# A transformer block's last stage: first inputs prepared in the stage before, inputs two tiles ahead, and the last tile turned on TensorE

## The chip, the cores and the metric

One core of a Trainium2 chip runs the whole program. Its engines have instruction streams of their own, each executed in order, and wait for one another by semaphores: TensorE (PE; its weight loads are shown apart as PEld), VectorE (DVE), ScalarE (ACT), GpSimd (POOL) and SyncE (SP), which here only issues DMAs. The metric is the device time of one execution in microseconds (us). Before the change it is 3047.3 us, the median of three runs (3041.62 to 3050.27).

## The reference

The input x has 128 sequences of 32 tokens with 512 features, 4096 tokens in all. Three residual steps follow one another, each on a layer norm of x: cross attention to 257 context rows, a delta-rule attention with a gated MLP, and a feed-forward network (FFN) on rotated and quantised values. The change lies in the last one. Its core:

```python
def act_quant(x):
    scale = 127.0 / jnp.clip(jnp.max(jnp.abs(x), axis=-1, keepdims=True), EPS)
    return jnp.clip(jnp.round(x * scale), -128.0, 127.0) / scale
def h_bitlinear(x, w):
    return jnp.einsum('bsh,oh->bso', act_quant(fwht(x)), weight_quant(w))
gate = h_bitlinear(hidden_states, w_gate)
up = h_bitlinear(hidden_states, w_up)
return h_bitlinear(jax.nn.silu(gate) * up, w_down)
```

fwht is a normalised Walsh-Hadamard rotation over the features (512 going in, 2048 before w_down); weight_quant gives weights of -1, 0 and 1 times one scale. The result is added to x.

## The kernel before

The program is a row of stages; intermediate results go through DRAM. Cross attention writes x1 and, beside its own work, the quantised FFN weights as bf16 (fq). The delta attention follows, then delta_out_mlp in 16 blocks of 256 tokens. Its function mlp makes gate and up products (L823, L826) and the down product (L834), adds the residual (L839) and stores x2 (L841). It also starts the FFN: it takes the mean off x2, applies the two upper levels of the rotation with additions (butterflies, L126 and L127) and stores the result as z2 (L846); the variance stays in mv2. A function solving(b) gives further work to deal out beside the MLP block b; it comes from beside_mlp, which hands out parts of the delta rule's substitution until they are used up. The function mixed deals out the steps of several lists by the share of their costs that is done. The function behind makes DVE instructions of such steps follow the MLP's last marked DVE instruction.

hadamard_ffn is the last stage, 32 tiles of 128 tokens. It opens its pools after the MLP: weights wg and wu (bf16, 16 KB a partition each) on the right side of SBUF, which the substitution used before, and wd beside them. PSUM has one pool of eight banks, named ps, for all products of the stage. One tile i goes through these steps:

- load brings z2 (tile zt, L932); turned transposes it on PE (L97, four 128x128 blocks) and copies it to SBUF on ACT (zT, L970);
- rotated multiplies each block with the 128x128 Hadamard matrix hd (L939), which ends the rotation;
- integers finds the largest magnitude (L976), makes the scale qs (L948, L950, L951), rounds by adding and subtracting a large constant (t on ACT, L956; q on DVE, L960) and makes the factors f (L981);
- integers_turned transposes q by a DMA from SP (qT, L986);
- middle computes, for each of four groups of 512 columns, the gate and up products (L996, L999), silu on ACT (s, L1001) and their product on DVE (m, L1002);
- butterflies applies the upper four levels of the 2048-wide rotation on DVE, eight operations of 128x1024;
- middle_turned transposes m on PE and copies it on ACT (mT, L1009); rotated follows for each group (four banks, pr);
- last_integers finds the maxima (L1016, L1020), the scale (L948 to L951), and rounds each group with two ACT operations (t L956, q L958); last_turned transposes q2 by DMA (q2T, L1031);
- finish makes the down product (L1037, bank pd), scales it on ACT (xo, L1039), adds x2 by an accumulating DMA from POOL (L1040) and stores the result from SP (L1041).

The loop over i interleaves tiles. In iteration i it does: load of tile i+3, turned of i+1, the first group of middle of i, rotated and integers of i+1, finish of i-3, the other three groups of middle of i, middle_turned, rotated and last_integers of i-1, and butterflies of i. Before the loop, tile 0 is turned, rotated, rounded and transposed. The planner of the framework takes this order as a priority; where an instruction isn't ready by its estimates, it puts a later one ahead of it on the same engine. So small DVE operations, which depend on one another, have butterflies of another tile between them.

Of the kernel before, what the change touches and what calls it, by code (L numbers as in the profile page):

```python
# [10 lines left out]
FP = mybir.dt.float32  # L11
BF = mybir.dt.bfloat16
# [684 lines left out]
def delta_out_mlp(  # L697
# [14 lines left out]
    with stack:  # L712
# [177 lines left out]
        for b in range(NBL):  # L890
            mixed(
                (3.5 * FC + 9.5 * NTL, mlp(b)),
                (16.0, back(b + 1) if b + 1 < NBL else None),
                (2.0, part(late, 2.0)),
                *((cost, behind(tc, mark, steps)) for cost, steps in solving(b)),
            )


def hadamard_ffn(g: Ctx, x2, z2, mv2, had, ffn, out):


    tc, nc = g.tc, g.nc
    c1, c2 = 1.0 / math.sqrt(D), 1.0 / math.sqrt(IF)
    NG = IF // D
    stack, (st, xp, wk1, mp1, wk, mp, ps) = pools(
        tc, ("d_st", 6), ("d_x", 4), ("d_wk1", 3), ("d_m1", 2), ("d_wk", 3), ("d_m", 2),
        ("d_ps", 8, PSUM),
    )
    right = dict(bufs=1, side="right", reuse_waits="tile")
    with tc.tile_pool(name="d_w", **right) as wp, tc.tile_pool(name="d_w2", **right) as wp2, stack:  # L910
        hd = wp.tile([P, P], FP, name="hd")
        nc.sync.dma_start(hd, had)
        w = []
        for i, (dst, sc) in enumerate(ffn):
            w.append(((wp, wp, wp2)[i].tile([P, IF * D // P], BF, name=f"wq{i}"), sc))
        (wg, sg), (wu, su), (wd, sd) = w
        for t, (dst, _) in zip((wg, wu), ffn):
            nc.sync.dma_start(t, dst)
        wg = wg.rearrange("p (c n) -> p c n", c=DC)
        wu = wu.rearrange("p (c n) -> p c n", c=DC)  # L920
        wd = wd.rearrange("p (c n) -> p c n", c=IC)
        magic = wp.tile([P, 1], FP, name="magic")
        nc.vector.memset(magic, MAGIC)
        minus = wp.tile([P, 1], FP, name="minus")
        nc.vector.memset(minus, -MAGIC)
        both = wp.tile([P, 2], FP, name="both")
        nc.vector.tensor_copy(both[:, 0:1], sg)
        nc.vector.tensor_copy(both[:, 1:2], su)

        def load(i, src, name):  # L930
            t = xp.tile([P, D], FP, name=name)
            nc.sync.dma_start(t, src[i * P : (i + 1) * P, :])  # L932
            return t

        def rotated(xT, c0):

            pr = ps.tile([P, D], FP, name="ps")
            for c in range(DC):
                nc.tensor.matmul(  # L939
                    pr[:, c * P : (c + 1) * P], xT[:, c0 + c, :], hd, start=True, stop=True  # L940
                )
            return pr

        def scales(mx, c):


            m = st.tile([P, 1], FP, name="m")
            nc.vector.tensor_scalar(m, mx, c, Q_EPS, ALU.mult, ALU.max)  # L948
            qs = st.tile([P, 1], FP, name="qs")
            nc.vector.reciprocal(qs, m)  # L950
            nc.vector.tensor_scalar(qs, qs, c, 127.0, ALU.mult, ALU.mult)  # L951
            return m, qs

        def rounded(q, pr, qs, scalar=False):
            t = wk.tile([P, D], FP, name="t")
            nc.scalar.activation(t, pr, AF.Identity, bias=magic, scale=qs)  # L956
            if scalar:
                nc.scalar.activation(q, t, AF.Identity, bias=minus)  # L958
            else:
                nc.vector.tensor_scalar(q, t, MAGIC, None, ALU.subtract)  # L960

        def statistics(ns):

            nc.scalar.activation(rstd[:, ns], mv2[:, ns, 1], AF.Sqrt, bias=g.ln_eps)
            nc.vector.reciprocal(rstd[:, ns], rstd[:, ns])
            nc.vector.tensor_scalar_mul(rstd[:, ns], rstd[:, ns], c1)

        def turned(i):
            zT = wk1.tile([P, DC, P], FP, name="zT")
            nc.scalar.copy(zT, g.transposed(ps, z.pop(i), g.ident))  # L970
            return zT

        def integers(i, pr):

            mx = st.tile([P, 1], FP, name="mx")
            nc.vector.tensor_reduce(mx, pr, AX.X, ALU.max, apply_absolute_value=True)  # L976
            m, qs = scales(mx, rstd[:, i : i + 1])
            q = wk1.tile([P, D], BF, name="q")
            rounded(q, pr, qs)
            f = st.tile([P, 2], FP, name="f")  # L980
            nc.vector.tensor_scalar_mul(f, both, m)  # L981
            return q, f

        def integers_turned(q, f):
            qT = wk1.tile([P, DC, P], BF, name="qT")
            nc.sync.dma_start_transpose(qT, q)  # L986
            return qT, f

        def middle(qT, f):

            m = mp.tile([P, IF], FP, name="m")
            for k in range(NG):
                ks = slice(k * D, (k + 1) * D)
                pg = ps.tile([P, D], FP, name="ps")
                for dc in range(DC):
                    nc.tensor.matmul(pg, qT[:, dc, :], wg[:, dc, ks], start=dc == 0, stop=dc == DC - 1)  # L996
                pu = ps.tile([P, D], FP, name="ps")
                for dc in range(DC):
                    nc.tensor.matmul(pu, qT[:, dc, :], wu[:, dc, ks], start=dc == 0, stop=dc == DC - 1)  # L999
                s = wk.tile([P, D], FP, name="s")  # L1000
                nc.scalar.activation(s, pg, AF.Silu, scale=f[:, 0:1])  # L1001
                nc.vector.scalar_tensor_tensor(m[:, ks], pu, f[:, 1:2], s, ALU.mult, ALU.mult)  # L1002
                yield m

        def middle_turned(m):
            mT = mp.tile([P, IC, P], FP, name="mT")
            for k in range(NG):
                pt = g.transposed(ps, m[:, k * D : (k + 1) * D], g.ident)
                nc.scalar.copy(mT[:, k * DC : (k + 1) * DC, :], pt)  # L1009
            return mT  # L1010

        def last_integers(pr):

            mx = st.tile([P, NG], FP, name="mx4")
            for k in range(NG):
                nc.vector.tensor_reduce(  # L1016
                    mx[:, k : k + 1], pr[k], AX.X, ALU.max, apply_absolute_value=True
                )
            mx1 = st.tile([P, 1], FP, name="mx")
            nc.vector.tensor_reduce(mx1, mx, AX.X, ALU.max)  # L1020
            mm, qs = scales(mx1, c2)
            q = mp1.tile([P, IF], BF, name="q2")
            for k in range(NG):
                rounded(q[:, k * D : (k + 1) * D], pr[k], qs, True)
            f = st.tile([P, 1], FP, name="fd")
            nc.vector.tensor_mul(f, mm, sd)
            return q, f

        def last_turned(q):
            qT = mp1.tile([P, IC, P], BF, name="q2T")  # L1030
            nc.sync.dma_start_transpose(qT, q)  # L1031
            return qT

        def finish(i, qT, f):
            pd = ps.tile([P, D], FP, name="ps")
            for c in range(IC):
                nc.tensor.matmul(pd, qT[:, c, :], wd[:, c, :], start=c == 0, stop=c == IC - 1)  # L1037
            xo = wk.tile([P, D], FP, name="xo")
            nc.scalar.activation(xo, pd, AF.Copy, scale=f)  # L1039
            nc.gpsimd.dma_start(xo, x2[i * P : (i + 1) * P, :], accum_op=ALU.add)  # L1040
            nc.sync.dma_start(out[i * P : (i + 1) * P, :], xo)  # L1041

        n = NT // P
        late = n - NTL
        rstd = wp.tile([P, n], FP, name="rstd")
        z = {i: load(i, z2, "zt") for i in range(3)}
        nc.sync.dma_start(wd.rearrange("p c n -> p (c n)"), ffn[2][0])
        statistics(slice(0, late))  # L1050
        f, m, q, done = integers_turned(*integers(0, rotated(turned(0), 0))), {}, {}, {}
        for i in range(n + 3):
            if i + 3 < n:
                z[i + 3] = load(i + 3, z2, "zt")
            if i + 1 < n:
                zT = turned(i + 1)
            if i < n:
                steps = middle(*f)
                m[i] = next(steps)
            if i == n // 2:  # L1060
                statistics(slice(late, n))
            if i + 1 < n:
                f = integers_turned(*integers(i + 1, rotated(zT, 0)))
            if 0 <= i - 3:
                finish(i - 3, *done.pop(i - 3))
            if i < n:
                for _ in steps:
                    pass
# [119 lines left out]
```

## Time and profile before

| what | us |
|---|---|
| median of three runs | 3047.3 (3041.62 to 3050.27) |
| profiled execution, its own time | 3042.59 |
| its span | 3040.8 |
| PE busy in the span | 2895.6 |
| DVE busy | 2010.3 |
| ACT busy | 1052.8 |
| POOL busy | 664.0 |

The profile comes from one execution. Busy time is the union of an engine's instructions; a matmul's end is modelled, so a full PE is not PE at its peak. A line number is that of the kernel's source; L97 is the helper transposed, and what it writes and reads tells which step it is. In a timeline row, start and duration stand first, then engine, line, operation, output and input with shapes; the bracket gives the idle time before it and what ended that. Rows of the same kind in a row are merged, with their count. The granted clock of PE is a share of full speed.

### The profile page before, as it was taken

The page shows a single profiled execution, that of the slowest core. Times are in us where ns is not written, and L with a number is a line of the kernel's source. Part 1 is how long each engine was busy: PE and PEld are TensorE (multiplying, and loading weights), DVE is VectorE, ACT ScalarE, POOL GpSimd, SP SyncE. Part 2 cuts the span into 40 slices and gives each one's busy share as a digit, 9 for nine tenths or more (in the row PEclk, how much of TensorE's full clock was granted, in tenths as well). Part 3 has the DMA queues.
Part 4 walks back from the last instruction along what each step waited for, and adds up shares of the span by engine and source line. Part 5 has one row for each costly group of instructions (what it writes and reads, how often), then busy time and mean ns, then how long its engine had stood idle before and what let it go on. Part 6 is the DMA issues. An engine that isn't in the chain of part 4 may idle for free.

```text
span 3040.8 us, 40815 instructions
## 1 busy us (share of the span) xinstructions
PE 2895.6 (95%) x14856; PEld 1647.0 (54%) x14918; DVE 2010.3 (66%) x3368; ACT 1052.8 (35%) x1780; POOL 664.0 (22%) x963
## 2 busy tenths in 40 slices
PE   8999999999999999599999999999999899999996
PEld 3444444443333333276666677776667666666664
DVE  2453534326699797368787877878522299989995
ACT  1111111215656666422111221112112156666664
POOL 1121212112686675321211110101000000000000
PEclk9999999999999999799999999999999999999998
DMA  9897998863554544641414132231311123344433
GB/s 331 278 309 267 320 308 311 281 215 96 170 147 128 174 132 123 200 137 58 132 54 127 57 119 82 74 99 42 128 52 46 56 60 77 77 82 83 82 66 65
DMA packets 344248, 428.99 MB, mean 141 GB/s; under 512 B 152304, under 2 KB 254832, under 8 KB 340592
## 3 DMA queue, kind: packets, MB, share of 16 engines
q1 hardware_dynamic: 307824, 326.19, 35.7%
q0 software_dynamic: 36224, 100.19, 10.8%
q8 instruction: 119, 1.95, 0.3%
q14 instruction: 81, 0.66, 0.1%
HBM read 288.36 MB, written 93.85 MB: 126 GB/s over the span
## 4 chain that ended last, share of the span: by engine, by line
PE 38%; issue 23%; DVE 4%; DMA 2%; POOL 1%; ACT 0%; SPq 0%; POOLq 0%; DVEq 0%; ACTq 0%
PE pm L823 8%; PE pm L826 8%; PE pm L834 8%; PE pp L520 5%; PE ps L797 4%; PE pg L455 2%; PE ps L764 2%; DVE W L442 1%; DVE pr L436 1%; DMA xs<-x 1%; POOL xo L1040 1%; DMA wd<-in_WdownT_dram 1%; PE ps L97 1%; PE pm L455 0%; PE pn L579 0%
## 5 line engine op out<-in xcount | busy, mean ns | idle before, releaser
L823 PE MATMUL pm<-hT,wg 128*128 128x256 f32 x1408 | 341.4, 385 | 0.7 <-ACT hT L812 0.7
L826 PE MATMUL pm<-hT,wu 128*128 128x256 f32 x1408 | 333.9, 380 | 0.0
L436 DVE TENSOR_TENSOR pr<-L,W 128x1984 f32<-128x1984 f32 (+30 forms) x248 | 311.3, 1255 | 25.0 <-DMA L<-ld 21.1
L442 DVE TENSOR_TENSOR W<-W,pr 128x1984 f32<-128x1984 f32 (+30 forms) x248 | 310.3, 1251 | 3.2
L834 PE MATMUL pm<-wd,mT 128*128 128x512 f32 x704 | 307.2, 592 | 0.0
L823 PEld LDWEIGHTS pm<-hT,wg 128*128 128x128 f32 x1408 | 261.7, 190 | 57.3 <-issue 16.0
L826 PEld LDWEIGHTS pm<-hT,wu 128*128 128x128 f32 x1408 | 267.4, 190 | 36.2
L834 PEld LDWEIGHTS pm<-wd,mT 128*128 128x128 f32 x704 | 132.6, 190 | 160.8 <-issue 160.7
L828 ACT ACTIVATE sg<-pm 128x256 f32<-128x256 f32 x176 | 67.3, 383 | 348.0 <-PE pm L823 333.2
L829 DVE TENSOR_TENSOR mT<-pm,sg 128x256 f32<-128x256 f32 x176 | 74.1, 421 | 164.0 <-PE pm L826 150.5
L1040 POOL DMA_DIRECT2D xo<-x x32 | 29.1, 908 | 589.1 <-ACT xo L1039 589.1
L956 ACT ACTIVATE t<-ps,magic,qs 128x512 f32<-128x512 f32 x160 | 117.5, 776 | 107.5 <-DVE qs L951 107.5
L996 PE MATMUL ps<-wq,qT 128*128 128x512 bf16 x453 | 124.3, 381 | 17.1 <-DMA qT<-q 15.3
L999 PE MATMUL ps<-wq,qT 128*128 128x512 bf16 x511 | 132.2, 381 | 1.5
L939 PE MATMUL ps<-hd,mT 128*128 128x128 f32 x1024 | 124.1, 280 | 9.9 <-ACT mT L1009 9.9
L461 POOL TENSOR_TENSOR kk<-kk,cm 128x256 f32<-128x256 f32 x128 | 132.8, 1038 | 2.1
L939 PEld LDWEIGHTS ps<-hd,mT 128*128 128x128 f32 x1024 | 118.7, 194 | 16.4 <-ACT mT L1009 16.1
L1037 PE MATMUL ps<-wq,q2T 128*128 128x512 bf16 x510 | 118.2, 385 | 9.2 <-DMA q2T<-q 9.0
L458 POOL DMA_DIRECT2D ld<-kk x128 | 92.5, 722 | 147.8 <-ACT kk L457 140.7
L455 PE MATMUL pg<-kqm,kq 128*32 128x512 f32 x896 | 118.8, 601 | 3.2 <-DMA kqm<-kq 2.5
L346 PE MATMUL ps<-hT,wq 128*128 128x512 f32 x256 | 113.7, 603 | 7.8 <-ACT hT L339 7.8
L302 PE MATMUL ps<-wo,aoT 128*128 128x512 f32 x256 | 117.0, 600 | 1.5 <-ACT aoT L295 1.5
(212 smaller groups left out, 5017.4 us busy)
## 6 DMA issues: line engine op xcount, KB each, us to landing
kall<-in_ctxT_dram SPq DMA_DIRECT2D x32, 2056.0 KB
cx<-in_ctx_dram SPq DMA_DIRECT2D x32, 2048.0 KB
x<-xo POOLq DMA_DIRECT2D x64, 256.0 KB, 3.5
ld<-kk POOLq DMA_DIRECT2D x128, 128.0 KB, 2.5
pd<-kk POOLq DMA_DIRECT2D x128, 128.0 KB, 2.3
L<-ld SPq DMA_DIRECT2D x8, 2048.0 KB
pe<-pd SPq DMA_DIRECT2D x256, 64.0 KB
kqm<-kq SPq DMA_DIRECT2D x448, 32.0 KB
```

The lines of the kernel that those rows point to most:

```text
L436: nc.vector.tensor_mul(pr[:, 0:n], bc(L[:, s, :, s + 1 : T].rearrange("p h t -> p t h"), HD), w[:, s].unsqueeze(1).to_broadcast([P, n, H4, ...
L442: nc.vector.tensor_sub(w[:, s + 1 :], w[:, s + 1 :], pr[:, 0:n])
L455: nc.tensor.matmul(pg[js], k[:, js], m[:, :, :, js], start=True, stop=True)
L461: nc.gpsimd.tensor_mul(kk[:, 1], kk[:, 1], cm.unsqueeze(1).to_broadcast([P, HH, T]))
L520: nc.tensor.matmul(pp.rearrange("p b t -> p (b t)"), w[n][:, dc, ec * P : (ec + 1) * P], hT[:, dc, :], start=dc == 0, stop=dc == DC - 1,)
L797: nc.tensor.matmul(pw, oT[:, i, dc, :], wo[:, dc, :], start=dc == 0, stop=dc == DC - 1)
L823: nc.tensor.matmul(pg, wg[:, dc, fs], hT[:, dc, :], start=dc == 0, stop=dc == DC - 1)
L826: nc.tensor.matmul(pu, wu[:, dc, fs], hT[:, dc, :], start=dc == 0, stop=dc == DC - 1)
L834: nc.tensor.matmul(pd, mT[:, fc, i * P : (i + 1) * P], wd[:, fc, :], start=fc == 0, stop=fc == FC - 1,)
L939: nc.tensor.matmul(pr[:, c * P : (c + 1) * P], xT[:, c0 + c, :], hd, start=True, stop=True)
L996: nc.tensor.matmul(pg, qT[:, dc, :], wg[:, dc, ks], start=dc == 0, stop=dc == DC - 1)
L999: nc.tensor.matmul(pu, qT[:, dc, :], wu[:, dc, ks], start=dc == 0, stop=dc == DC - 1)
```

## The change

The stage becomes a class, HadamardFfn, that is made before the attention stages. Its method open allocates the right-side pool, loads hd, wg and wu and makes the constants; it is called where block 14 of the MLP is planned, after the substitution's pool is given back. Its method first turns, rotates, rounds and transposes tiles 0 and 1, in six steps dealt out beside block 15, the last one; it uses the MLP stage's PSUM pool and single buffers z0, z0T and q0. Its method run is the rest. In its loop, turned and integers now concern tile i+2, loads run further ahead, and the transposing DMA is issued from integers before f is made. finish of i-3 moves from between the first and second group of middle to after middle_turned. For the last tile (end) each rounded group of q2 is transposed on PE in bf16, subtraction and copies alternate between DVE and ACT, and finish adds x_end, loaded before, in one DVE operation, with no accumulating DMA. The pool of m, mT and mb goes to the right side, wd behind it.

```diff
-                *((cost, behind(tc, mark, steps)) for cost, steps in solving(b)),
+                *((cost, behind(tc, mark, steps)) for cost, steps in solving(b, ps)),
...
+    def integers(self, i, pr, st, q, qT, t):
+        nc = self.nc
+        mx = st.tile([P, 1], FP, name="mx")
+        nc.vector.tensor_reduce(mx, pr, AX.X, ALU.max, apply_absolute_value=True)
+        m, qs = self.scales(st, mx, self.rstd[:, i : i + 1])
+        self.rounded(q, t, pr, qs, False)
+        nc.sync.dma_start_transpose(qT, q)
+        f = st.tile([P, 2], FP, name="f")
+        nc.vector.tensor_scalar_mul(f, self.both, m)
+        self.ready[i] = qT, f
...
+    def open(self, ctx):
+        tc, nc = self.tc, self.nc
+        wp = self.wp = ctx.enter_context(tc.tile_pool(name="d_w", **self.right))
+        self.hd = wp.tile([P, P], FP, name="hd")
+        nc.sync.dma_start(self.hd, self.had)
+        (_, sg), (_, su), _ = self.ffn
+        w = [wp.tile([P, IF * D // P], BF, name=f"wq{i}") for i in range(2)]
+        for t, (dst, _) in zip(w, self.ffn):
             nc.sync.dma_start(t, dst)
...
+    def first(self, ps):
+        nc, wp = self.nc, self.wp
+        self.statistics(slice(0, NT // P - NTL))
+        for i in range(2):
+            z = wp.tile([P, D], FP, name="z0")
+            nc.sync.dma_start(z, self.z2[i * P : (i + 1) * P, :])
+            yield 1
+            zT = wp.tile([P, DC, P], FP, name="z0T")
+            nc.scalar.copy(zT, self.g.transposed(ps, z, self.g.ident))
+            yield 1
+            q = wp.tile([P, D], BF, name="q0")
+            qT = wp.tile([P, DC, P], BF, name=f"q0T{i}")
+            self.integers(i, self.rotated(ps, zT, 0), wp, q, qT, z)
+            yield 1
...
+        mpool = tc.tile_pool(name="d_m", **{**self.right, "bufs": 2})
+        stack, (st, xp, wk1, wk, mp1, ps) = pools(
+            tc, ("d_st", 6), ("d_x", 4), ("d_wk1", 3), ("d_wk", 3), ("d_m1", 2), ("d_ps", 8, PSUM),
+        )
+        with mpool as mp, tc.tile_pool(name="d_w2", **self.right) as wp2, stack:
...
+            def last_integers(pr, end):
...
+                for k in range(NG):
+                    ks = slice(k * D, (k + 1) * D)
+                    scalar = not end or k % 2 == 1
+                    self.rounded(q[:, ks], wk.tile([P, D], FP, name="t"), pr[k], qs, scalar)
+                    if end:
+                        pt = g.transposed(ps, q[:, ks], g.identb, BF)
+                        copy = nc.scalar.copy if k % 2 else nc.vector.tensor_copy
+                        copy(qT[:, k * DC : (k + 1) * DC, :], pt)
+                if not end:
+                    nc.sync.dma_start_transpose(qT, q)
...
+                if i == n - 1:
+                    nc.vector.scalar_tensor_tensor(xo, pd, f, x_end, ALU.mult, ALU.add)
+                else:
+                    nc.scalar.activation(xo, pd, AF.Copy, scale=f)
+                    nc.gpsimd.dma_start(xo, self.x2[rows, :], accum_op=ALU.add)
+                nc.sync.dma_start(self.out[rows, :], xo)
...
+            for i in range(2, 6):
+                load(i)
+            nc.sync.dma_start(wd.rearrange("p c n -> p (c n)"), wd_dram)
+            m, done = {}, {}
+            for i in range(n + 3):
+                if i + 2 < n:
+                    zT = turned(i + 2)
+                if 0 < i and i + 5 < n:
+                    load(i + 5)
+                if i < n:
+                    steps = middle(*self.ready.pop(i))
+                    m[i] = next(steps)
+                if i == n // 2:
+                    self.statistics(slice(late, n))
+                if i + 2 < n:
+                    integers(i + 2, rotated(ps, zT, 0))
+                if i < n:
+                    for _ in steps:
+                        pass
+                if 0 <= i - 1 < n:
+                    mT = middle_turned(m.pop(i - 1))
+                if 0 <= i - 3:
+                    finish(i - 3, *done.pop(i - 3))
+                if i == n - 1:
+                    x_end = xp.tile([P, D], FP, name="zt")
+                    nc.sync.dma_start(x_end, self.x2[i * P :, :])
+                if 0 <= i - 1 < n:
+                    pr = [rotated(ps, mT, k * DC) for k in range(NG)]
+                    done[i - 1] = last_integers(pr, i == n)
+                if i < n:
+                    m[i] = butterflies(nc, m[i], mp.tile([P, IF], FP, name="mb"))
...
-        def beside_mlp(b):
-
-            return [(PACE, part(all_u, PACE))]
+        def beside_mlp(b, ps):
+
+
+            if b < NT // TB - 2:
+                return [(PACE, part(all_u, PACE))]
+            if b == NT // TB - 2:
+                assert next(all_u, None) is None
+                lent.close()
+                ffn.open(right)
+                return []
+            return [(6.0, ffn.first(ps))]
...
-    hadamard_ffn(g, x2, z2, mv2, had, list(zip(fq, scales)), out)
+        ffn.run()
```

## The prediction

> **What bounds the kernel now.** I read the page first (TensorE busy 95% of the span), then busy time by stretches, since the change touches only the last quarter: the handover from the MLP to the rotated FFN at 2410, the FFN's 32 tiles, and its end. Columns: stretch and length, busy us of PE, PEld, DVE, ACT, POOL, clock, DMA share, GB/s.
>
> ```profile
> 2330.00:2400.00 70.00, 69.32 (x256) 47.59 (x255) 13.76 (x33) 9.31 (x19) 3.45 (x5) 1.00 0.04 16
> 2400.00:2480.00 80.00, 65.45 (x332) 41.40 (x336) 57.81 (x104) 34.56 (x54) 3.06 (x5) 0.89 0.25 73
> 2720.00:2800.00 80.00, 77.89 (x476) 50.80 (x484) 72.72 (x118) 47.31 (x79) 3.68 (x4) 1.00 0.39 84
> 2960.00:3041.00 81.00, 55.06 (x296) 34.28 (x299) 44.09 (x70) 35.92 (x59) 4.31 (x5) 0.85 0.31 64
> ```
>
> PE has 14.6 us idle in the handover row and 26 in the last; in the MLP DVE and ACT are nearly free; in the tiles PE and DVE are both over 90% busy. The timeline of the handover:
>
> ```profile
> 2410.00 0.60 PE L97 MATMUL ps<-ident,zt 128*128 128x128 f32 x4
> 2416.15 0.43 DVE L960 TENSOR_SCALAR q<-t 128x512 bf16<-128x512 f32 x1 [0.91 <-ACT t L956]
> 2421.58 0.13 PEld L996 LDWEIGHTS <-qT 128*128 128x128 bf16 x2 [8.95 <-DMA qT<-q]
> ```
>
> MLP ends at 2410.0. Tile 0 is then turned, rotated, rounded (2416.6) and turned by DMA; the first gate matmul comes at 2421.99, after 9.1 us in which PE stands. In the steady part the period is 18.25 us (rotations of mT start at 2700.70, 2718.95, 2737.20). One period of the timeline gives the loop that sets it:
>
> ```profile
> 2718.95 3.84 PE L939 MATMUL ps<-hd,mT 128*128 128x128 f32 x32 [0.23 <-ACT mT L1009]
> 2722.83 0.69 DVE L1016 TENSOR_REDUCE mx<-ps 128x1 f32<-128x512 f32 x1 [0.20 <-PE ps L939]
> 2728.29 0.15 DVE L951 TENSOR_SCALAR qs<-qs 128x1 f32<-128x1 f32 x1
> 2728.47 1.45 ACT L956 ACTIVATE t<-ps,magic,qs 128x512 f32<-128x512 f32 x2 [3.66 <-DVE qs L951]
> 2734.82 1.86 ACT L1001 ACTIVATE s<-ps,f 128x512 f32<-128x512 f32 x3
> 2736.53 2.09 ACT L1009 COPY mT<-ps 128x512 f32<-128x512 f32 x4
> ```
>
> Rotation to the last maximum 4.57; to qs 4.92, because butterflies of the next tile stand between the small operations; four (t, q) pairs on ACT 5.15, to 2733.59; xo 0.57, t 0.66, three s 1.71, first mT copy 0.68 until the next rotation. Sum 18.26: it closes without slack, over ACT's order. PE's own work, start to start, is 3.68 (rotation) + 0.44 + 1.72 + 0.89 + 3.46 (finish) + 5.19 + 1.83 (turns of m) = 17.2; DVE's 72.7/80 x 18.25 = 16.6. The waits of 2500 to 2960 (25 tiles; total, times, longest) say how much the change's two targets are:
>
> ```profile
> DVE q L960 <- ACT t L956: 29.5, 25, 1.2
> PE ps L939 <- ACT mT L1009: 8.7, 23, 0.4
> PE ps L996 <- DMA qT<-q: 3.3, 5, 0.9
> ```
>
> So qT is late in few tiles, and those tiles take 18.25 us like the others.
>
> **The skill.** The Trainium skill, "TensorE: Matmul & The Clock Gate", Part 1 (What's actually happening): after an idle window the array runs at half clock for some microseconds. The trace agrees: from 2421.99 gate matmuls start 0.43 us apart until about 2425, later 0.216. "VectorE: DVE Perf Modes", The three transpose paths: a 128x128 bf16 turn costs 390 ns on TensorE against 1309 ns by DMA, and TensorE's lands in PSUM; here four f32 turns took 0.60 us, and the DMA turn of q2 5.7 us to its first use. "DMA: Bandwidth & Descriptors", Anatomy of one DMA: about 2 us of every DMA is fixed, mostly the write's receipt; the accumulating DMA at the end took 4.3. "Perfetto Trace Analysis", Identifying Performance Opportunities: equal bubbles can mean that PSUM has run out; in some periods the turns of m wait for ACT's xo, t and s (0.3, 0.3, 0.2 us), which hold the eight banks.
>
> **The change, part by part.** Sums are against the profiled execution: 3042.6 us, span 3040.8; the median of the runs is 3047.3, 4.7 above it.
>
> *Handover.* Two turns (0.44 to 0.60 each) and two rotations (0.89 to 1.05) go into the MLP's last block, 57 us in which PE is full: it ends 3.1 later, at 2413.1. Their DVE and ACT work (0.69 + 0.43 and four small operations, 1.9 in all, and 0.59 + 0.78 a tile) is covered by engines at 20% and 13%; uncovered, it would be these 10 us. The square root's table load (1.28) was in this block already. The weights are no new cover: their DMAs were issued at 2176 before too; the wd load and the z loads still follow. The two z loads on SP meet an almost idle queue (16 GB/s). A turn of z that waits for its load would hold PE, in order: I take 0, bound 0 to 3 (the x stores land in 3.5). Tile 1 uses tile 0's single buffers again; the steps are dealt out over the block, six in 57 us, so some 9 us lie between them. Then tile 2's turn 0.5, gate and up k=0 1.72, rotation 0.89, three more pairs 5.2 at full clock, and 0.95 to the product: m of tile 0 is whole at 2422.3, against 2432.5. Gain 10.2.
>
> *Integers two ahead.* qT gets a period more; the wait was 3.3 us in all on PE, in a loop that didn't pass through it: 0 on its own. On SP, an out store that waits for xo's DMA holds what is behind it for up to 4.4 us: after the change that is q2T's turn, used some two periods later, then z loads and the next qT's turn, used a period later; if that slack were gone it would be those 4.4 a tile. q on DVE still waits 1.2 for ACT's t, with the products behind it.
>
> *finish after the turns of m.* Its 3.46 us fill the 0.4 in which PE waits for mT; xo (0.57) leaves the ACT loop, since it now runs where ACT waits for qs. The same 3.46 no longer stand between gate pair 0 and pair 1, so pair 1 ends 8.5 us after the rotation starts (3.68 + 0.44 + 1.72 + 0.89 + 1.73) instead of 12.0, and its s can run on ACT ahead of the (t, q) pairs: another 0.6 out. Loop: 18.26 - 0.57 - 0.6 = 17.1, under PE's 17.2; DVE with q's wait unfilled 16.6 + 1.2 = 17.8. Against that, finish now lies between turns and rotation, where late banks push it onto the loop. Bounds 17.2 to 19.6; I take 18.0: 0.25 x 30 periods = 7.5.
>
> *End.* Before: first t at 3014.02, then:
>
> ```profile
> 3017.91 1.33 ACT L958 ACTIVATE q<-t,minus 128x512 bf16<-128x512 f32 x2
> 3019.27 1.91 SPq L1031 DMA_TRANSPOSE q2T<-q  x1
> 3024.94 6.17 PE L1037 MATMUL ps<-wq,q2T 128*128 128x512 bf16 x16 [9.05 <-DMA q2T<-q]
> 3031.14 0.69 ACT L1039 ACTIVATE xo<-ps,fd 128x512 f32<-128x512 f32 x1 [11.32 <-PE ps L1037]
> 3032.12 0.85 POOL L1040 DMA_DIRECT2D xo<-x  x1 [11.17 <-ACT xo L1039]
> ```
>
> The last store is issued at 3036.4 and the span ends 4.4 later. After: ACT does four t (0.72) and two q (0.66), 4.2, with one copy (0.6) between; last turn 0.7 and copy 0.8: 3020.3, with the matmuls starting at 3019.6. Sixteen take 3.5 at full clock, 6.2 at half: to 3023.1 or 3025.8. A sum on DVE (0.75, priced by the product row) replaces xo, POOL's DMA and its landing; store 4.4. End 3028.6 to 3031.3: gain 9.5 to 12.2, taken 11. x_end is loaded in iteration 31 and used in iteration 34, hidden.
>
> Sum: 10.2 + 7.5 + 11 = 28.7; 3042.6 - 28.7 = 3013.9, and on the median's footing 3018.6: I say 3018.
>
> **Rivals.**
> (1) *PE becomes the bound.* For: the loop above falls to 17.1. Against: DVE in order with 1.2 of wait. At 17.5, 0.75 x 30 = 22.5, with 21.2 of both ends: about 3004.
> (2) *Finish on the loop; slower.* If only s of pair 1 gets ahead of the (t, q) pairs, four pr banks, prz and the pairs behind hold all eight; the last turn and pd get theirs from t and s after the pairs. Loop: 9.5 to qs, 5.15, t 0.66, s 0.65, finish 3.46, signals 0.2 = 19.6. For: qs came 9.5 after the rotation, with butterflies always at hand to stand before it. Against: products come earlier too, so fewer butterflies may be left, and a PE idle before the turns would take finish first. 1.35 x 30 = 40.5, less 21.2: 3066. It decides above 18.25 + 21.2/30 = 18.96 us a period.
> (3) *The period stays 18.25*, as the loop only changes places: the ends' 21.2 alone, 3026.
> (4) *The handover doesn't gain* because PE waits in the MLP for z, zT or a bank: 7 to 10 less.
>
> **How the numbers follow.** About 0.3% (9 us) is what a measurement of this kernel can tell from no change. Forecast with (3), periods of 17.8 to 18.5: 0.40, 3010 to 3033. (1): 0.24, 2998 to 3010. Periods of 18.7 to 19.25, or (4) with a period just longer: within 0.3%, 0.12. (2): 0.24, 3056 to 3070. Faster 0.64, same 0.12, slower 0.24. A range of 3000 to 3060 leaves out the bottom of (1) and over half of (2); the likeliest case's own is 3010 to 3033.
>
> **What would show it.** Right: PE's first gate matmul under 1 us after the MLP's last, near 2413; no wait of PE on qT; rotations of mT 17.8 to 18.5 apart; no DMA turn and no POOL DMA for the last tile, and some 6 us from its first t to its first down matmul, where 10.9 were. Wrong: rotations 19 or more apart, with the turns of m waiting for ACT's s or t and finish right behind them: then (2) holds. If the MLP's last block grows by more than 4 us, (4).

## The result, and the profile after

The changed kernel takes 3037.0 us (median; 3032.2 to 3045.1), the kernel before, run beside it, 3041.4: a ratio of 0.9982 with a 95% interval of 0.9973 to 0.9991. That is 5.5 us of the 28.7 that the prediction summed up. The profiled executions are 3042.59 (span 3040.8) and 3032.95 (span 3031.2) and differ by 9.6, more than those 5.5, since the changed kernel's profile comes from one of the three fastest of its 22 executions. In the changed kernel's profile L835 to L1041 have other numbers: rotated is L917, the scale L927 to L930, t and q L935 and L937 or L939, gate and up L1032, s L1036, m L1037, the down products L1077, xo L1082.

First the busy time by stretches of the changed kernel, the same stretches and columns as before (stretch and length, busy us of PE, PEld, DVE, ACT, POOL, clock, DMA share, GB/s):

```profile
2330.00:2400.00 70.00, 69.76 (x273) 49.11 (x272) 16.39 (x40) 11.03 (x22) 3.44 (x5) 1.00 0.06 21
2400.00:2480.00 80.00, 73.11 (x399) 46.80 (x399) 70.46 (x124) 39.45 (x62) 3.06 (x5) 0.96 0.31 84
2720.00:2800.00 80.00, 76.32 (x457) 47.92 (x455) 70.99 (x119) 50.45 (x83) 3.39 (x4) 1.00 0.37 76
2960.00:3031.20 71.20, 53.32 (x306) 33.48 (x303) 41.47 (x68) 34.48 (x56) 3.39 (x4) 0.92 0.30 63
```

The handover has 6.9 us of idle PE where it had 14.6, at a clock of 0.96 in place of 0.89. The steady stretch has gone the other way: 3.7 us idle in 80, where it had 2.1. The timeline of the handover:

```profile
2409.59 0.60 PE L97 MATMUL ps<-ident,zt 128*128 128x128 f32 x4
2410.03 1.89 PE L1032 MATMUL ps<-wq,q0T 128*128 128x512 bf16 x8
```

The MLP's last matmul is followed at once by a turn and by the first gate product; the wait for qT is gone. One long period of the tiles:

```profile
2712.22 3.73 PE L917 MATMUL ps<-hd,mT 128*128 128x128 f32 x32
2720.98 0.15 DVE L930 TENSOR_SCALAR qs<-qs 128x1 f32<-128x1 f32 x1
2721.23 1.44 ACT L935 ACTIVATE t<-ps,magic,qs 128x512 f32<-128x512 f32 x2 [0.63 <-DVE qs L930]
2726.34 0.68 ACT L1036 ACTIVATE s<-ps,f 128x512 f32<-128x512 f32 x1
2727.08 0.66 PE L97 MATMUL ps<-ident,m 128*128 128x128 f32 x4 [0.46 <-ACT s L1036]
2727.75 3.61 PE L1077 MATMUL ps<-wq,q2T 128*128 128x512 bf16 x16
2731.20 3.73 PE L917 MATMUL ps<-hd,mT 128*128 128x128 f32 x32
```

The rotations of mT here stand 18.98 us apart. Read downwards, the rows are the loop, that is, the chain of work and waits that leads from one rotation to the next: 8.91 to the end of qs, 0.1 to t, 5.11 for the four pairs t and q, 0.74 for an s on ACT, which gives the last turn of m its PSUM bank, 0.67 for that turn, 3.45 for finish; together 18.98. The waits of 2500 to 2960 (total, times, longest) say the same. Before, no turn of m had an entry for PE in that view:

```profile
DVE q L939 <- ACT t L935: 47.6, 16, 3.0
PE ps L97 <- ACT t L935: 15.2, 24, 1.2
PE ps L97 <- ACT s L1036: 4.1, 9, 0.5
```

Over the stretch the starts of the rotations repeat in threes, 17.50, 18.98 and 19.42 apart, with two of 21.0. In those of 19.42 the last turn waits 1.23 us for a t, in those of 17.50 the turns of m don't wait. The mean over periods 4 to 28 is 18.78 (18.25 before). The end:

```profile
3011.21 2.11 ACT L935 ACTIVATE t<-ps,magic,qs 128x512 f32<-128x512 f32 x3 [3.17 <-DVE qs L930]
3015.89 0.61 PE L97 MATMUL ps<-identb,q 128*128 128x128 bf16 x4 [0.87 <-ACT q L937]
3016.30 8.56 PE L1077 MATMUL ps<-wq,q2T 128*128 128x512 bf16 x32
3024.89 0.75 DVE L1080 SCALAR_TENSOR_TENSOR xo<-ps,fd,zt 128x512 f32<-128x512 f32 x1 [9.41 <-PE ps L1077]
```

The DMA turn and the accumulating DMA of the last tile are gone, but 32 matmuls stand behind the last turn, not 16: finish of tile 30 has been placed ahead of finish of tile 31. From the first t to the end it is 20.0 us, before 26.8.

Where the 9.6 us come from: in the MLP's last but one block the second half of the down products begins 2.6 us earlier (2339.67 against 2342.31); this shift is older than PE's work on tiles 0 and 1, since the block before has it too (2260.05 against 2262.68). From there to the end of tile 0's fourth product it is 11.1 us less (2418.85, where it was 2432.54, less those 2.6). From there to the start of the rotation of tile 31's mT it is 11.8 more (587.04 against 575.26). From that rotation to the end it is 7.7 less (25.3 against 33.0), of which 6.8 lie behind the first t. 2.6 + 11.1 - 11.8 + 7.7 = 9.6.

### The profile page after: what moved, and what is told of

Read it like the earlier page. It is cut to its first block, busy times and chain, and to the rows that moved or that the text cites. A ratio compares the mean times of both kernels' runs of the same rounds, so it can differ in the third digit from the quotient of the medians.

```text
span 3031.2 us, 40875 instructions
## 1 busy us (share of the span) xinstructions
PE 2896.5 (96%) x14934; PEld 1647.3 (54%) x14934; DVE 2002.5 (66%) x3373; ACT 1055.8 (35%) x1779; POOL 659.2 (22%) x962
## 4 chain that ended last, share of the span: by engine, by line
PE 48%; DVE 10%; ACT 5%; issue 2%; DMA 1%; POOL 0%; SPq 0%; ACTq 0%; DVEq 0%; POOLq 0%
PE pm L823 9%; PE pm L826 9%; PE pm L834 9%; PE pp L520 5%; PE ps L797 4%; ACT t L935 2%; PE ps L917 2%; PE ps L1077 2%; ACT q L937 2%; PE ps L1032 2%; PE ps L764 2%; PE pg L455 2%; DVE mb L126 2%; PE ps L97 2%; DVE mx L1051 1%
## 5 line engine op out<-in xcount | busy, mean ns | idle before, releaser
L1032 PE MATMUL ps<-wq,qT 128*128 128x512 bf16 x960 | 218.7, 379 | 0.3
L1032 PEld LDWEIGHTS <-qT 128*128 128x128 bf16 x960 | 93.7, 98 | 103.0 <-issue 4.6
L935 ACT ACTIVATE t<-ps,magic,qs 128x512 f32<-128x512 f32 x158 | 115.9, 777 | 19.5 <-DVE qs L930 19.3
L917 PEld LDWEIGHTS ps<-hd,mT 128*128 128x128 f32 x1024 | 119.6, 192 | 4.3
L1077 PE MATMUL ps<-wq,q2T 128*128 128x512 bf16 x512 | 120.6, 391 | 0.5 <-ACT t L935 0.3
L917 PE MATMUL ps<-hd,mT 128*128 128x128 f32 x1024 | 119.7, 275 | 0.0
L520 PE MATMUL pp<-hT,wk 128*128 128x512 f32 x256 | 117.6, 600 | 0.7 <-DVE acc L527 0.4
```

The lines of the kernel that those rows point to most:

```text
L520: nc.tensor.matmul(pp.rearrange("p b t -> p (b t)"), w[n][:, dc, ec * P : (ec + 1) * P], hT[:, dc, :], start=dc == 0, stop=dc == DC - 1,)
L917: self.nc.tensor.matmul(pr[:, c * P : (c + 1) * P], xT[:, c0 + c, :], self.hd, start=True, stop=True)
L935: nc.scalar.activation(t, pr, AF.Identity, bias=self.magic, scale=qs)
L1032: nc.tensor.matmul(p, qT[:, dc, :], w[:, dc, ks], start=dc == 0, stop=dc == DC - 1)
```

## The experiments

"Period" is the mean distance between rotations of mT, periods 4 to 28 of the profiled execution. The letters of the theories are defined in each text on record.

| run | edit | ratio to before (95%) | period |
|---|---|---|---|
| change | | 0.9982 (0.9973 to 0.9991) | 18.78 |
| e1 | change, finish at its old place | 0.9931 (0.9915 to 0.9947) | 18.24 |
| e2 | before, finish at the new place | 1.0046 (1.0030 to 1.0061) | 18.71 |
| e3 | change, finish of tile 30 ahead of the last rounding | 0.9959 (0.9945 to 0.9973) | 18.71 |
| e4 | e1 and e3 together | 0.9912 (0.9894 to 0.9930) | 18.25 |
| e5 | e4, xo after the copies of mT | 0.9849 (0.9832 to 0.9865) | 17.68 |
| e6 | e4, two of four q on VectorE | 0.9849 (0.9832 to 0.9866) | 17.39 |
| e7 | e4, tiles 0 and 1 not beside the MLP | 0.9944 (0.9928 to 0.9960) | 18.24 |
| e8 | e4, integers one tile ahead | 0.9903 (0.9887 to 0.9919) | 18.24 |
| e9 | change, two of four q on VectorE | 0.9916 (0.9902 to 0.9929) | 17.94 |
| e10 | e5, one of four q on VectorE | 0.9833 (0.9819 to 0.9846) | 17.44 |
| e11 | e4, butterflies behind qs | 0.9786 (0.9767 to 0.9806) | 17.01 |
| e12 | change, butterflies behind qs | 0.9899 (0.9883 to 0.9914) | 17.79 |

**e1 and e2: the place of finish.** One takes this single part out of the change, the other puts it alone into the kernel before.

```diff
                 if i + 2 < n:
                     integers(i + 2, rotated(ps, zT, 0))
+                if 0 <= i - 3:
+                    finish(i - 3, *done.pop(i - 3))
                 if i < n:
                     for _ in steps:
                         pass
                 if 0 <= i - 1 < n:
                     mT = middle_turned(m.pop(i - 1))
-                if 0 <= i - 3:
-                    finish(i - 3, *done.pop(i - 3))
```

> The changed kernel with the finish of tile i-3 put back between the first and the second group of the middle; the weights, the first two tiles, integers two ahead and the end stay changed. Theory A (finish between the turns of m and the rotation put its 3.46 us on the loop over ACT and the PSUM banks): the rotations of mT come 18.25 us apart again instead of 18.8 on average, and the whole gets some 12 us faster than the changed kernel, to 0.994 of the kernel before. Theory B (making integers two tiles ahead lengthens the period, since its bank is held longer and its t stands behind the last integers on ACT): periods stay at 18.6 or more, and the time at 0.998.

> The kernel before with one edit: finish of tile i-3 comes after the turns of m. Theory A: periods of 18.6 to 19.0 instead of 18.25, and 10 to 20 us slower than before (1.003 to 1.007). Theory B: the period stays at 18.25 or gets shorter by up to 0.5, since PE no longer waits for mT; 0.995 to 1.000.

Measured: with finish back the rotations stand 18.24 to 18.25 apart again, and the ratio falls from 0.9982 to 0.9931, 15.5 us; 30 x (18.78 - 18.25) is 15.9. The kernel before with finish after middle_turned has the changed kernel's repeating 17.50, 18.98 and 19.42 (and one of 21.0), and is slower than before by 0.46%, 14.0 us; 30 x (18.71 - 18.25) is 13.8. Its waits of PE are those of the changed kernel too:

```profile
PE ps L97 <- ACT t L956: 14.9, 24, 1.2
```

So the longer period comes from the place of finish, and from no other part of the change.

**e3 and e4: the end.**

```diff
-                if 0 <= i - 3:
+                if 0 <= i - 3 and i != n + 1:
                     finish(i - 3, *done.pop(i - 3))
...
                     pr = [rotated(ps, mT, k * DC) for k in range(NG)]
+                    if i == n:
+                        finish(n - 2, *done.pop(n - 2))
                     done[i - 1] = last_integers(pr, i == n)
```

> The changed kernel with finish of tile 30 issued before the last tile's rounding, not behind its turns. If the end gained less than forecast because these 16 matmuls (3.5 us at full clock, up to 4.7 measured) stand behind the last turns and ahead of the last 16: 3 to 4.5 us less from the last tile's first t to the end, 0.9988 of the changed kernel. If instead the last tile's turns and copies set the end: no change there.

> Both edits of the two kernels above, finish back in its place and finish of tile 30 early. Theory A and the tail's explanation together: period 18.25 and an end some 11 us shorter than before; with 10 at the handover that is 21 to 24 us, 0.992 to 0.993 of the kernel before. Theory B: 0.997.

Measured in e3: the first t of the last tile is at 3013.64, finish of tile 30 runs at 3012.24 beside the maxima, and the span ends at 3028.7: 15.1 us from that t on, where the changed kernel has 20.0. These 4.9 are a little more than the 3 to 4.5 expected. The timeline of e3:

```profile
3019.33 5.11 PE L1077 MATMUL ps<-wq,q2T 128*128 128x512 bf16 x16
3024.47 0.75 DVE L1080 SCALAR_TENSOR_TENSOR xo<-ps,fd,zt 128x512 f32<-128x512 f32 x1 [6.98 <-PE ps L1077]
```

Sixteen matmuls are left behind the last turn, 5.1 us, and 4.2 lie between the start of the sum and the end. Against the kernel before this end gains 26.8 - 15.1 = 11.7. e4 has both edits and a ratio of 0.9912, 26.8 us below the kernel before, with the old period; 21 to 24 were expected.

**e5 and e6: is the 18.25 ScalarE's loop?** Two ways to take work out of ACT's order between qs and the copy of mT. In e5 finish is cut: the matmuls stay (down), and xo with its DMAs follows the copies of mT. In e6, in every tile, scalar is true for the second and fourth group alone.

```diff
-                    finish(i - 3, *done.pop(i - 3))
+                    part_done = down(i - 3, *done.pop(i - 3))
...
                     mT = middle_turned(m.pop(i - 1))
+                if 0 <= i - 3 and i != n + 1:
+                    finish(*part_done)
```

```diff
-                    scalar = not end or k % 2 == 1
+                    scalar = k % 2 == 1
```

> The kernel of e4 with finish cut in two: its 16 matmuls stay between the first and the second group of middle, its scaling xo on ScalarE and the two DMAs follow the copies of mT. Theory A (the 18.25 us period is the loop over ScalarE's order: four pairs t and q, xo, t, three s, first copy of mT, then the rotation): xo's 0.57 us leaves the loop, rotations of mT come about 17.7 apart, and the time is about 16 us below e4's ratio of 0.9912, near 0.986. Theory C (the period is PSUM's eight banks or TensorE's own work): pd's bank is held some 8 us longer, the rotations stay 18.25 apart or come later, ratio 0.991 or more.

> The kernel of e4, where in every tile, not only in the last, the subtraction q of the first and third group of q2 is made by VectorE instead of ScalarE. Theory A: two q (0.66 us each) leave ScalarE's loop, 18.25 - 1.3 = 16.9, so TensorE's 17.2 or VectorE decides; VectorE gains 2 x 0.43 = 0.86 on 16.6, 17.5 without idle time. Period 17.3 to 17.8, ratio 0.983 to 0.987. Theory D (VectorE in order is as near a bound as ScalarE): q's waits for t stand in front of products and butterflies, qs comes later, period 18.3 to 19, ratio 0.992 to 0.999.

Measured: e5's period is 17.68, 0.57 below 18.25, which is xo's 0.57, though pd keeps its bank longer. e6's is 17.39, in the range; its periods repeat 17.96, 17.13 and 17.11. Both ratios are 0.9849, 19 us below e4. So at 18.25 the loop ran over ACT, and neither PE's own work nor the banks were the bound.

**e7 and e8: the two parts ahead of the loop.** e7 calls first at the beginning of run, ahead of the loads, and leaves the last MLP block alone. e8 prepares only tile 0 there and has i + 1 in turned and integers.

```diff
-            return [(6.0, ffn.first(ps))]
+            return []
...
+            for _ in self.first(ps):
+                pass
             for i in range(2, 6):
                 load(i)
```

> The kernel of e4, with tiles 0 and 1 turned, rotated, rounded and turned by DMA at the beginning of the FFN stage and not beside the MLP's last block; the weights hd, wg and wu are still loaded at block 14. If the handover is worth what the two traces show (11.1 us, of which 9 are TensorE standing before the first gate matmul), the time rises by 9 to 12 us against e4, to a ratio near 0.9948. If the difference of those traces was variation before the FFN, it stays near 0.9912.

> The kernel of e4 with turned and integers one tile ahead, as in the kernel before; beside the MLP's last block only tile 0 is prepared. If two tiles ahead are worth nothing in a loop that doesn't pass through qT (the prediction), the ratio stays at 0.991 (0.990 to 0.9925) and rotations of mT 18.25 apart. If the wait for qT costs, up to 0.9 us in some tiles, the time rises by 3 to 10 us, ratio 0.992 to 0.9945.

Measured: e7 is 9.7 us above e4 (0.9944 against 0.9912, intervals that barely touch). In its timeline the MLP's last matmul ends at 2411.8 and the first gate product starts at 2427.25, 15.4 us later, where the kernel before has 12.0. There is one wait of 8.45 us between them for the z of tile 1, which has to follow tile 0 through the single buffers:

```profile
2422.68 1.12 PE L97 MATMUL ps<-ident,z 128*128 128x128 f32 x4 [8.45 <-DMA z<-z]
2427.25 2.29 PE L1032 MATMUL ps<-wq,q0T 128*128 128x512 bf16 x8
```

So e7's handover is not quite that of the kernel before. In the profiled executions the stretch from the last but one block's down products to tile 0's fourth product is 13.2 us longer in e7 than in e4 (102.2 against 89.1), and 3.2 of these come back before tile 31. The 10.0 that remain are near the 11.1 that the traces of before and after showed. e8 is the same as e4 within the intervals, and its period is 18.24: with finish at its old place, two tiles ahead are worth nothing that can be measured.

**e9 and e10: the same cut in the changed kernel, and both cuts together.** e9 is e6's edit in the changed kernel, with finish at the new place. e10 is e5 with q of the third group on VectorE.

> The changed kernel (finish after the turns of m) with one edit: in every tile the subtraction q of the first and third group of q2 is made by VectorE. Theory A' (the longer period of the changed kernel, 18.6 to 18.8 on average, runs through ScalarE's four pairs t and q, whose end frees the bank for the last turn of m, with finish behind it): two q (0.66 us each) leave that loop, so the rotations of mT come 17.3 to 17.6 apart on average, near TensorE's 17.2, the waits of the turns of m for t all but vanish, and the time is 1.1 to 1.4 x 30 = 33 to 42 us below the changed kernel, ratio 0.984 to 0.988. Rival B (finish at the later place costs by itself, by a bank that pd takes or by matmuls at half clock, whatever ScalarE does): the period stays above 18.2, ratio 0.994 or more.

> The kernel of e5 (finish cut in two, period 17.68) with the subtraction q of the third group on VectorE. If the period of e5 is still ScalarE's loop, it falls by 0.66 to about 17.05, which is what TensorE needs by the shortest distances of e6 (17.04 to 17.1); VectorE's work rises from 16.5 to 16.9. Period 17.05 to 17.3, ratio 0.979 to 0.982, faster than both e5 and e6. If TensorE or VectorE already decides in e5, the period stays at 17.5 or more and the ratio at 0.984 or more.

Both missed. e9's period fell by 0.84, not by 1.3: 17.94 is above the 17.3 to 17.6 that theory A' gave and below the 18.2 of rival B, so neither came out as written. One of its periods of 18.03:

```profile
2794.70 3.73 PE L917 MATMUL ps<-hd,mT 128*128 128x128 f32 x32
2803.94 0.15 DVE L930 TENSOR_SCALAR qs<-qs 128x1 f32<-128x1 f32 x1
2804.95 2.75 PE L1032 MATMUL ps<-wq,qT 128*128 128x512 bf16 x12 [0.79 <-ACT t L935]
2807.53 1.91 PE L97 MATMUL ps<-ident,m 128*128 128x128 f32 x16
2809.28 3.62 PE L1077 MATMUL ps<-wq,q2T 128*128 128x512 bf16 x16
2812.73 3.73 PE L917 MATMUL ps<-hd,mT 128*128 128x128 f32 x32
```

It is 9.39 to the end of qs, 0.86 until a t on ACT has freed a bank, 2.58 for the gate and up products that waited for it, 1.75 for the turns of m and 3.45 for finish: 18.03. The turns no longer wait, but the wait for a bank has moved ahead to the products, and finish still stands behind it. e6, with the same q on VectorE and finish at its old place, has 17.39, or 0.55 less; e1 had 0.54 less than the changed kernel. So taking work out of ACT shortens either loop but leaves what the place of finish costs, and in this rival B was nearer than theory A'. The half clock that rival B named is not the reason: e9's granted clock was 1.00 from 2500 to 2940.

e10 has 17.44 on average, with periods from 17.1 to 17.66, in which qs ends 8.95 to 10.06 us after the rotation's start. It is no clear gain on e5, since the intervals overlap. In both runs qs came later on average: 9.47 us after the rotation's start in e9, where the changed kernel has 9.25, and 9.59 in e10, where e5 has 9.49. That took back a part of what ACT had given, and the rest of the shortfall lies behind qs. The time from the rotation to qs, which I had taken as given, is not fixed.

**e11 and e12: the butterflies ahead of qs.** From the last maximum to qs there are four dependent operations of 0.15 us each, and VectorE puts three or four butterflies of 1.22 us between them, and in some periods a product of 0.74. The kernel before, from the end of the last maximum at 2723.52 to qs at 2728.29:

```profile
2723.44 1.22 DVE L127 TENSOR_TENSOR mb<-m 128x1024 f32<-128x1024 f32 x1
2724.57 0.15 DVE L1020 TENSOR_REDUCE mx<-mx 128x1 f32<-128x4 f32 x1
2724.69 1.23 DVE L126 TENSOR_TENSOR m<-mb 128x1024 f32<-128x1024 f32 x1
2725.83 0.15 DVE L948 TENSOR_SCALAR m<-mx 128x1 f32<-128x1 f32 x1
2725.89 1.22 DVE L127 TENSOR_TENSOR m<-mb 128x1024 f32<-128x1024 f32 x1
2727.03 0.16 DVE L950 RECIPROCAL qs<-m 128x1 f32<-128x1 f32 x1
2727.10 0.14 DVE L1026 TENSOR_TENSOR fd<-m,sc 128x1 f32<-128x1 f32 x1
2727.16 1.22 DVE L126 TENSOR_TENSOR mb<-m 128x1024 f32<-128x1024 f32 x1
```

Both runs hold the upper three levels behind qs of the tile before; e11 with finish at the old place, e12 with the changed kernel's.

```diff
-                    m[i] = butterflies(nc, m[i], mp.tile([P, IF], FP, name="mb"))
+                    a, b, step = m[i], mp.tile([P, IF], FP, name="mb"), 1
+                    for level in range(4):
...
+                            if level >= 1 and i > 0:
+                                es.enter_context(tc.issue_after(self.last_qs))
+                            nc.vector.tensor_add(dst[:, :, 0, :], src[:, :, 0, :], src[:, :, 1, :])
+                            nc.vector.tensor_sub(dst[:, :, 1, :], src[:, :, 0, :], src[:, :, 1, :])
```

> The kernel of e4 with one edit: on VectorE the upper three of the four levels of butterflies of tile i (six of eight operations of 1.22 us) are held behind qs of last_integers of tile i-1, so that the four small operations from the maxima to qs follow one another. Theory A (the period is a loop from the rotation over VectorE's qs, ScalarE's pairs and copies, and back): qs comes about 5.5 us after the rotation's start in place of 9.5, the loop falls to about 14.7 and no longer decides; TensorE's 17.05 to 17.2 does. Period 17.05 to 17.4, ratio 0.978 to 0.983. Rival E (the butterflies have to be done before the turns of m anyway, VectorE in order is the loop): period 18.0 or more, ratio 0.99 or more.

> The changed kernel with the same one edit, finish after the turns of m as it was. Theory A': with qs 4 us earlier the four pairs t and q end before the turns of m need their banks, so finish stands behind nothing late: period 17.05 to 17.5 where the changed kernel has 18.6 to 18.8, some 40 us below the changed kernel, ratio 0.983 to 0.988. Rival B (finish at the later place costs by itself): period 18.2 or more, ratio 0.995 or more.

Measured in e11, a row of the timeline and one of busy time by stretches:

```profile
2711.67 0.15 DVE L930 TENSOR_SCALAR qs<-qs 128x1 f32<-128x1 f32 x1
```

```profile
2720.00:2800.00 80.00, 80.00 (x519) 54.94 (x518) 77.53 (x131) 53.92 (x90) 3.39 (x4) 1.00 0.41 88
```

The rotation before that qs starts at 2706.59: qs ends 5.2 us later, not 8.9 to 9.5. PE is busy for all of the 80 us, no wait of PE is listed in 2500 to 2940, and the period is 17.01, just under the 17.05 to 17.4 expected. That TensorE is now the bound is read from this; no run took work off it from here. The ratio is 0.9786, 38 us below e4; 30 x (18.25 - 17.01) is 37. At a median of 2978.8 us e11 beats both kernels and is the fastest of all that ran.

e12 missed by 0.3: 17.79. Its timeline:

```profile
2702.67 3.73 PE L917 MATMUL ps<-hd,mT 128*128 128x128 f32 x32
...
2707.74 0.15 DVE L930 TENSOR_SCALAR qs<-qs 128x1 f32<-128x1 f32 x1
...
2714.97 2.20 PE L97 MATMUL ps<-ident,m 128*128 128x128 f32 x16 [0.34 <-DVE m L1127]
2717.01 3.62 PE L1078 MATMUL ps<-wq,q2T 128*128 128x512 bf16 x16
2720.46 3.73 PE L917 MATMUL ps<-hd,mT 128*128 128x128 f32 x32
```

qs is as early as in e11, and ACT's pairs are off the loop. But the turns of m now wait 0.34 us for the last butterflies (L1127), 12.3 us after the rotation's start, and finish stands behind them again: 12.30 + 2.04 + 3.45 = 17.79. The 0.78 us between e11 and e12 are the cost of finish's place with this loop, as the 0.5 between e1 and the change are with the other: whichever loop ends in the turns of m, finish behind them is on it.

## Why the prediction was wrong

3037 lies in the range, but the forecast of 3018 rested on a shorter period, and the period became longer.

- **Handover: right.** Predicted 10.2 us, measured 11.1 in the traces, and 9.7 by e7 against e4, whose handover is a little worse than that of the kernel before. The MLP's block grew by about 2.2 us (its end hardly moved, 2410.0 to 2409.6, though it began 2.6 earlier) where 3.1 were taken, and its sign, a first gate product right behind the MLP, was seen. Rival (4) didn't come.
- **Integers two ahead: right,** 0, by e8, at the old place of finish.
- **Finish after the turns of m: this is the step that failed,** in its sign. It took a period of 18.0 for a gain of 7.5; it became 18.78, 11.8 us lost between tile 0's product and tile 31's rotation. What the step named did happen: in the period shown, xo (2712.94) runs beside the wait for qs and s of pair 1 (2719.91) ahead of the first t (2721.23). But its sum, 18.26 - 0.57 - 0.6, took those two out of the loop and put finish in at nothing, on the ground that finish fills the 0.4 us in which PE waits for mT. In the trace the last turn of m gets its bank only after the pairs, and then the turn and all of finish, 0.67 + 3.45, are on the loop. The step wrote this down ("where late banks push it onto the loop") and weighed it too low. That the turn waits for a bank is read from what released it, an s or a t that had read PSUM; the number of banks was not varied.
- **Rival (2), finish on the loop: right in mechanism, too large.** It gave 19.6 a period and 3066 in all. The loop it summed is the one in the timeline: 9.5 to qs was 8.91, 5.15 was 5.11, t and s were one operation of 0.74 and not two of 1.31, 0.67 for the last turn it had left out, finish 3.46 was 3.45. That is 18.98 for this order of the tiles; the others of the three give 17.50 and 19.42. With 18.78 the loss is 15.5 us by e1, while the two ends gained 11.1 + 7.7 = 18.8 in the traces, where 21.2 were taken: a small gain remains where rival (2) foresaw a loss. That the time fell inside the stated range is this balance, not the forecast mechanism.
- **End: right in kind, the sum short of one item.** Predicted 11, measured 6.8 from the first t on. (The terms that it names add up to an end at 3028.3, not 3028.6.) The matmuls started 5.1 us after the first t (5.6 predicted), but there were 32. The prediction didn't ask where finish of tile 30 would go once the last tile had no DMA turn to wait for. e3 shows the item by taking it away: 4.9 us, and the gain is then 11.7.
- **Rival (1), PE as the bound,** was the right limit and needed another edit: 17.2 was worked out for PE's own work, and e11 reaches 17.01.

What would have told it beforehand is the sum of rival (2), which has finish in it and came to 19.6 from the rows of before. Beside this, the prediction had the row with qs 9.5 us behind the rotation and said that butterflies stood between the small operations, but it treated that half of the loop as fixed. It was the largest term and, by e11, the one that could be taken away.

That the orders of VectorE and ScalarE come in threes in the changed kernel is what the trace shows; why the planner settles on three was not tried.

## What to carry to other kernels

When an instruction is moved on an engine that works in order, sum the loop twice, once with it at each place, and count banks: behind a step that waits for a buffer its whole length is on the loop through that wait, though its engine had idle time; here 3.45 us, which made the period 0.54 longer than the loop that had set it before. In a loop that closes over several engines, look for the longest stretch made of small dependent operations with other work dealt in between; here holding that work back by 4 us was worth 38 us, more than the whole change. And where the last item of a pipeline becomes faster, check what is now queued between it and the end.

## What the runs showed of the hardware

After the same short waits PE's granted clock mostly stayed full and sometimes fell to half. In one of the two periods of 21.0 us of the changed kernel, and in a period of 19.42:

```profile
2633.18 0.77 PE L97 MATMUL ps<-ident,m 128*128 128x128 f32 x4 [1.23 <-ACT t L935]
2633.76 5.22 PE L1077 MATMUL ps<-wq,q2T 128*128 128x512 bf16 x16
...
2746.59 0.66 PE L97 MATMUL ps<-ident,m 128*128 128x128 f32 x4 [1.23 <-ACT t L935]
2747.17 3.61 PE L1077 MATMUL ps<-wq,q2T 128*128 128x512 bf16 x16
```

In the first, after idle times of 0.24 and 1.23 us for banks, finish took 5.22 us and not 3.61; the granted clock was 0.50 from 2633.6 to 2637.0 and 0.92 over the period (2617.8 to 2638.8), and 1.00 in the periods on either side. The second has the same two waits at full clock. Between 2500 and 2940 this pair of waits stands in eight periods each of the changed kernel, e2 and e3, and in two, one and one of them it fell; in all other runs, without the pair, the granted clock in that stretch was 1.00. What decides in which of the 24 it falls, the runs don't show. The Trainium skill, "TensorE: Matmul & The Clock Gate", A second HAM failure mode: psum-queue depth-cycling, describes short idling between groups of matmuls that cycle through PSUM banks, frequent enough to make the clock swing between half and full. The same page's Part 1 (What's actually happening) ties half clock to an idle window of about 3.4 us; the trace has it after much shorter waits, and the trace decides. Periods with waits of 0.43 and 0.46 us kept the full clock.

Time before the FFN differs between executions of kernels that have that part in common, by several us: the first rotation of mT began at 2432.8 in the profile of e5 and at 2443.8 in that of e4. Differences of stages were therefore taken within an execution, and those between kernels from the ratios.
